# Moving the last block's output layer, its norms and the first GELU in a three-layer hybrid kernel

## The chip, the cores and the metric

The kernel runs on one core of a Trainium2 chip. A core has five engines that run at the same time, each through its own queue of instructions in a fixed order: TensorE (PE, with the loading of weights, PEld, shown apart), VectorE (DVE), ScalarE (ACT), GpSimd (POOL) and SyncE (SP), which here issues DMAs. An instruction waits for the results of others through semaphores, and whatever stands behind it on its engine waits with it.

The metric is the device time of one execution in microseconds (us), lower is better; several executions are timed and the median is given. One more execution is recorded by the hardware profiler.

## The reference

The input `x` has 4 sequences of 1024 tokens with 256 channels, in float32. Three layers follow, each added to `x`: a linear recurrent unit (LRU), a latent attention, and a sparse feed-forward layer that is applied before the attention and once more at the end. What the change touches is the end of the LRU and the beginning of the first sparse layer.

The end of the LRU, for one block of tokens (cut from the reference):

```python
out = out2[0] - out2[1] + o
y = gelu(out @ w1_w + w1_b)
y = y @ w2_w + w2_b + out
mean, var = y.mean(-1), y.var(-1)
y = (y - mean) * rsqrt(var + LN_EPS) * ln_g + ln_b      # then x = x + y
```

The sparse layer norms each token of `x` and takes a small grouped convolution of it (256 channels to 64); the result is normed a second time, over all 4096 tokens, by channel:

```python
xc = einsum('ngf,gf->ng', x2d.reshape(n, g, 4), conv_w) + conv_b
mean, var = xc.mean(0), ((xc - mean) ** 2).mean(0)
xa = gelu((xc - mean) * rsqrt(var + BN_EPS) * gamma + beta)
logits = xa @ lin_w.T + lin_b
```

Of the logits, made into weights by an exponential, each token keeps the largest (a top-k), once for its inputs and once for its outputs, around a dense product with a 256x256 matrix. The mean and variance over all tokens make a barrier: no GELU, and so no top-k, can start before the last token's convolution is done.

## The kernel before

The 4096 tokens lie in SBUF as 8 blocks of 512, each of 4 tiles of 128 tokens (32 tiles, `x[i]`). The program is written with a tile framework: its text gives the instructions and a priority by their order, and a scheduler sets the order on each engine from that and from a model of their durations. `tc.issue_after(ins)` adds a dependency by hand.

The stages lie in this order on the time axis. The LRU takes to about 257 us. For every block `Lru.outputs` makes the products `po` (L437, TensorE, moved by ACT to `ot`), the gate's first product `pz` (L443) with its GELU on ACT, the second product with its sum `ot` on VectorE (L455), the transposes `py` (L465, back to tokens on partitions), and the layer norm of `py`, after which the result is added to `x`. `layer_norm` (L124) takes `bn_stats` and `bn_aggr` of each view, then a reciprocal root by `rsqrt` on VectorE (L55 to L66: a guess by integer arithmetic and three Newton steps, tiny instructions one behind the other), and at last `shift` = -mean x rstd (L136). The normed value `yn` is one ACT instruction per tile with that scale and shift (L474); then `yn` x gain and `x` + `yn` (L479, L480), on GpSimd for most blocks. The last block is done in two halves of 256 tokens, to shorten the end, with these two on VectorE (`bufs` is set only there).

Beside the LRU run the heads of the first sparse layer, `Ffn.head` (L501), one for each block: `layer_norm` of `x`, then `normalized_t` (`xn` on ACT, L145, and its transposes `pt` on TensorE, L147), a copy `ft` of these (ACT, L524), its store to DRAM by SP (L527), the convolution `pc` (L529), `xc` (ACT, L533), and its statistics (VectorE, L534). The heads of blocks 0 to 3 lie in the LRU's loop. For the end of the loop the text has: head of block 4; three steps of the halves of the last block; head of block 5; the other steps; head of block 6 behind the last GELU of the LRU; and the two half heads of block 7 side by side.

Then `norm_scale` (L538) gathers the statistics of all blocks and makes from them scale `bs` and bias `bt` (tiny VectorE instructions, with the same root, L59 to L66). `gelu` (L585) is one ACT instruction per block of 512 tokens. `logits_product` (L551) gives `pl` for one tile, and `Ffn.tile` (L589) the top-k: MAX8 and MATCH_REPLACE8 on VectorE, in turns, all under the line L674, their order fixed by hand. The product with the dense matrix `pf` (L567, `full_product`) reads `tt`, the block's stored `ft`, loaded back by L561; later blocks make it ahead of time (`ahead`, `pfa`). The second product (`px`, L682, and L699) is made from the gated `xg` (L657, L658) and added to `x` (L662). `wfs` are the dense matrix in two parts for the more exact products later: a cast on ACT (L1151) and a difference on GpSimd (L1152). The weights of the attention (`attn_weights`, `wd`, `wqk`) are prepared beside the first tiles.

The first sparse layer's tiles 0 to 7 take 281 to 336 us. The attention, with tiles 8 to 31 of the first sparse layer and the heads of the second between its products, follows to about 1304 us, and the tiles of the second sparse layer end the run.

Of the kernel before, what the change touches and what calls it, by code (L numbers as in the profile page):

```python
# [10 lines left out]
F32 = mybir.dt.float32  # L11
# [5 lines left out]
ALU = mybir.AluOpType  # L17
# [4 lines left out]
P = 128  # L22
# [98 lines left out]
    return c, s, last  # L121


def layer_norm(nc, pool, tag, views, rstd=None, shift=None):  # L124

    n = len(views)
    mv = pool.tile([P, n, 2], F32, tag=f"{tag}_mv", name=f"{tag}_mv")
    if rstd is None:
        both = pool.tile([P, 2, n], F32, tag=f"{tag}_rs", name=f"{tag}_rs")
        rstd, shift = both[:, 0, :], both[:, 1, :]  # L130
    for i, v in enumerate(views):
        st = pool.tile([P, 6], F32, tag=f"{tag}_st", name=f"{tag}_st", bufs=4)
        nc.vector.bn_stats(st, v)
        nc.vector.bn_aggr(mv[:, i, :], st)
    rsqrt(nc, pool, tag, mv[:, :, 1], rstd)
    nc.vector.scalar_tensor_tensor(shift, mv[:, :, 0], -1.0, rstd, ALU.mult, ALU.mult)  # L136
    return rstd, shift


def normalized_t(nc, pool, psum, tag, ptag, views, rstd, shift, ident):  # L140

    pt = psum.tile([P, KD, len(views) * P], ptag, "pt")
    for i in range(len(views)):
        xn = pool.tile([P, D], F32, tag="fx_xn", name="xn", bufs=2)
        nc.scalar.activation(xn, views[i], AF.Identity, bias=shift[:, i : i + 1], scale=rstd[:, i : i + 1])  # L145
        for k in range(KD):
            nc.tensor.transpose(pt[:, k, i * P : (i + 1) * P], xn[:, k * P : (k + 1) * P], ident)  # L147
    return pt
# [46 lines left out]
class Lru:  # L195
# [226 lines left out]
    def outputs(self, r, xs, xnt, h, pairs, last, tag="po", bufs=None):  # L422

        nc, w, sp, vecs = self.nc, self.w, self.sp, self.vecs
        tiles = range(2 * pairs[0], 2 * pairs[-1] + 2)
        sl = slice(tiles[0] * P, (tiles[-1] + 1) * P)
        n = len(tiles) * P
        ot, zt = bufs or self.buffers()
        for c in range(KD):
            co = slice(c * P, (c + 1) * P)  # L430
            po = self.psum.tile([P, 512], tag, "po")[:, 0:n]
            self.inputs(po, r, 2, c, xnt, sl, stop=False)
            terms = [
                (self.w_mid[r][k][e][:, co], h[k][e][:, sl.start + r : sl.stop + r]) for k in range(KD) for e in range(2)
            ]
            for i, (lt, v) in enumerate(terms):
                nc.tensor.matmul(po, lt, v, start=False, stop=(i == len(terms) - 1))  # L437
            nc.scalar.activation(ot[:, c, :], po, AF.Identity, bias=self.ob[:, r, c : c + 1])
            yield
        for c in range(KD):  # L440
            pz = self.psum.tile([P, 512], "pu", "pz")[:, 0:n]
            for k in range(KD):
                nc.tensor.matmul(  # L443
                    pz, w[:, k, 2, c * P : (c + 1) * P], ot[:, k, :], start=(k == 0), stop=(k == KD - 1)
                )
            last_gelu = nc.scalar.activation(zt[:, c, :], pz, AF.Gelu, bias=vecs[:, V_B1 + c : V_B1 + c + 1])
        self.last_gelu = last_gelu.ins
        yield
        for c in range(KD):
            pz = self.psum.tile([P, 512], tag, "pz2")[:, 0:n]  # L450
            for k in range(KD):
                nc.tensor.matmul(
                    pz, w[:, k, 3, c * P : (c + 1) * P], zt[:, k, :], start=(k == 0), stop=(k == KD - 1)
                )
            nc.vector.scalar_tensor_tensor(  # L455
                ot[:, c, :], pz, vecs[:, V_B2 + c : V_B2 + c + 1], ot[:, c, :], ALU.add, ALU.add
            )
        yield
        pys = []
        for j in range(len(tiles) // 2):  # L460
            py = self.psum.tile([P, 2, D], "pu" if tag == "pu" else "py", "py")
            for i in range(2):
                tk = slice((2 * j + i) * P, (2 * j + i + 1) * P)
                for k in range(KD):
                    nc.tensor.transpose(py[:, i, k * P : (k + 1) * P], ot[:, k, tk], self.ident)  # L465
            pys += [py[:, 0, :], py[:, 1, :]]
        rstd, shift = layer_norm(nc, sp, f"ly{len(tiles)}", pys)
        gain, base = self.brow[:, 0, :], self.brow[:, 1, :]
        for q, tile_q in enumerate(tiles):
            xt = xs[tile_q]  # L470
            yn = sp.tile([P, D], F32, tag="yn", name="yn", bufs=3)
            if last:
                nc.gpsimd.tensor_tensor(xt, xt, base, ALU.add)
            self.last_yn = nc.scalar.activation(  # L474
                yn, pys[q], AF.Identity, bias=shift[:, q : q + 1], scale=rstd[:, q : q + 1]
            ).ins
            if last:
                engine = nc.vector if bufs else nc.gpsimd
                engine.tensor_tensor(yn, yn, gain, ALU.mult)  # L479
                engine.tensor_tensor(xt, xt, yn, ALU.add)  # L480
            else:
                nc.gpsimd.tensor_tensor(yn, yn, gain, ALU.mult)
                nc.gpsimd.tensor_tensor(yn, yn, base, ALU.add)
                nc.gpsimd.tensor_tensor(xt, xt, yn, ALU.add)
        yield


class Ffn:
# [9 lines left out]
        self.counted = 0  # L498
        self.dram, self.turned, self.full = None, {}, {}

    def head(self, blk, sp, psum, ptag, pairs=(0, 1), xtag="fx", ttag="ft"):  # L501


        nc, w = self.nc, self.w
# [14 lines left out]
        for i, j in enumerate(pairs):  # L519
            r = slice(2 * j, 2 * j + 2)  # L520
            xs = self.x[blk * 4 + 2 * j : blk * 4 + 2 * j + 2]
            pt = normalized_t(nc, sp, psum, xtag, ptag, xs, norm[:, 0, r], norm[:, 1, r], w.ident)
            tt = sp.tile([P, KD, 256], F32, tag=ttag, name="ft", bufs=2 if self.dram else 1)
            nc.scalar.copy(tt, pt)  # L524
            yield
            if self.dram:
                nc.sync.dma_start(self.turned[blk][:, :, j * 256 : (j + 1) * 256], tt)  # L527
            for k in range(KD):
                nc.tensor.matmul(  # L529
                    pc[k * 64 : (k + 1) * 64, i * 256 : (i + 1) * 256], w.cw[:, k, :], tt[:, k, :], start=True, stop=True  # L530
                )
# [6 lines left out]
    def norm_scale(self, sp):  # L538

        nc, w = self.nc, self.w  # L540
        bmv = sp.tile([P, 2], F32, tag="bmv", name="bmv")
        nc.vector.bn_aggr(bmv, self.bst[:, 0 : self.counted, :].rearrange("p a b -> p (a b)"))
        bs = self.bp.tile([P, 1], F32, tag="bs", name="bs", bufs=2)
        rsqrt(nc, sp, "bn", bmv[:, 1:2], bs)
        nc.vector.tensor_tensor(bs, bs, w.vecs[:, V_GAMMA : V_GAMMA + 1], ALU.mult)
        bt = self.bp.tile([P, 1], F32, tag="bt", name="bt", bufs=2)
        nc.vector.tensor_tensor(bt, bmv[:, 0:1], bs, ALU.mult)
        nc.vector.tensor_tensor(bt, w.vecs[:, V_BETA : V_BETA + 1], bt, ALU.subtract)
        self.bs, self.bt = bs, bt

    def logits_product(self, dst, i):  # L551
        nc, w = self.nc, self.w
# [29 lines left out]
            nc.sync.dma_start(self.full[blk][:, 2 * j : 2 * j + 2, :], v)  # L582
            yield

    def gelu(self, blk):  # L585
        x = self.xc[blk]
        return self.nc.scalar.activation(x, x, AF.Gelu, bias=self.bt, scale=self.bs).ins  # L587

    def tile(self, i, sp, psum, tags, out=None, fast=False, parts=None, tt=None, fine=False):  # L589
# [395 lines left out]
def run(*gens):  # L985
    for g in gens:
        for _ in g:
            pass
# [58 lines left out]
def tile_kernel(ctx: ExitStack, tc: tile.TileContext, x_in, w_lru, vecs_in, rows, w_ffn, lin_t, w_attn, w_down, out):  # L1047
# [34 lines left out]
    with ExitStack() as c1:  # L1082
# [16 lines left out]
        for k in range(NBLK):  # L1099
# [25 lines left out]
                h[b].append(lru.states(xnt[b * CH : (b + 1) * CH], c))  # L1125
            if 2 <= k < NBLK - 2:
                run(f1.head(k - 2, lru.sp, psum, "pt"))
        for blk in range(4, NBLK - 3):
            run(f1.head(blk, lru.sp, psum, "pt"))
        k = NBLK - 1  # L1130
        ot, zt = lru.buffers()
        halves = [
            lru.outputs(k % CH, xb[k], xnt[k], h[k // CH], (i,), last, tag, [v[:, :, c : c + 256] for v in (ot, zt)])
            for i, tag, c in ((0, "pu", 0), (1, "po", 256))
        ]
        for i in (0, 0, 1):
            next(halves[i])
        run(f1.head(NBLK - 3, lru.sp, psum, "pt"))
        for i in (0, 1, 0, 1, 0, 1, 1):
            next(halves[i])  # L1140
        with tc.issue_after(lru.last_gelu):
            run(f1.head(NBLK - 2, lru.sp, psum, "pt"))
        run(*(f1.head(NBLK - 1, lru.sp, psum, "pu", (i,), "lx", "zt") for i in range(2)))

    with ExitStack() as c2:
        sp = c2.enter_context(tc.tile_pool(name="at_s", bufs=2))
# [2 lines left out]
        wqk, wvo, wd = two([P, KD, HEADS * HD], "wqk"), two([P, PAIRS, D], "wvo"), two([P, KD, P], "wd")  # L1149
        wfs = two([P, KD, D], "wf")  # L1150
        nc.scalar.copy(wfs[0], w.wf)  # L1151
        nc.gpsimd.tensor_tensor(wfs[1], w.wf, wfs[0].bitcast(F32), ALU.subtract)  # L1152
        at = Attention(tc, x, ident, ident64, wqk, wvo, wd, sp, wp)
        with ExitStack() as c4:
            psum = Banks(
# [1 line left out]
            )  # L1157
            fp = c4.enter_context(tc.tile_pool(name="f_t", bufs=4))
            weights = attn_weights(nc, fp, psum, "at", w_attn, w_down, wqk, wvo, wd, at, ident64)
            f1.norm_scale(sp)  # L1160
            tts = [f1.load(blk, fp, f"tt{blk}") for blk in range(2)]
            f1.gelu(0)
            with tc.issue_after(f1.gelu(1)):
                warm(nc, sp, AF.Exp)
            tiles = [
# [174 lines left out]
```

## Time and profile before

| | us |
|---|---|
| median of 3 runs | 1511.01 (1509.11 to 1512.66) |
| profiled execution | 1507.37 |
| its span, first instruction to last | 1505.6 |
| mean granted TensorE clock in it | 0.952 of full speed |

A row of the timeline gives the start from the span's start, the length, the engine, the line of the kernel, the operation, and what it writes and reads with the shape; `x4` says that the row stands for four such instructions, and a bracket at the end how long the engine had been idle before and what released it. These rows are the middle of the end of the LRU (second half of the last block), from its last sum to the statistics of `x`:

```profile
255.34 0.47 DVE L455 SCALAR_TENSOR_TENSOR ot<-pz,vecs,ot 128x256 f32<-128x256 f32 x1
255.41 1.01 PE L465 MATMUL py<-ident,ot 128*128 128x128 f32 x4 [0.37 <-DVE ot L455]
...
256.45 0.76 DVE L133 BATCH_NORM_STATS2 ly_st<-py 128x6 f32<-128x256 f32 x2
...
260.95 1.02 ACT L474 ACTIVATE yn<-py,ly_rs 128x256 f32<-128x256 f32 x2
...
262.95 0.42 DVE L480 TENSOR_TENSOR x<-x,yn 128x256 f32<-128x256 f32 x1
...
263.68 0.42 DVE L133 BATCH_NORM_STATS2 fx_st<-x 128x6 f32<-128x256 f32 x1
...
266.08 1.09 ACT L145 ACTIVATE xn<-x,norm_f 128x256 f32<-128x256 f32 x2 [0.30 <-DVE norm_f L136]
```

In the table of windows a row gives a stretch and its length, the busy time of PE, PEld, DVE, ACT and POOL with the number of instructions, the granted clock of TensorE, the busy share of the DMA engines, and GB/s.

### The profile page before, as it was taken

What the parts mean: (1) busy time and instruction counts of PE and PEld (TensorE: products, weight loads), DVE (VectorE), ACT (ScalarE), POOL (GpSimd) and SP (SyncE); (2) the same over time, 40 slices, a digit from 0 to 9 for tenths busy, and PEclk for the clock granted to TensorE, in tenths of its full rate; (3) what the DMA queues carried; (4) which work ended last, traced back from release to release, by engine and by line L of the source; (5) the groups of instructions that cost most, each with busy time, mean ns of one, the idle gap of its engine ahead of it and who ended that gap; (6) DMA issues with size and microseconds to landing.
All of it is one profiled execution on the core that took longest, in us unless ns stands there. A gap on an engine that the chain in (4) does not pass through costs nothing. (4 is left out here: it accounts for less than half of the span.)

```text
span 1505.6 us, 28728 instructions
## 1 busy us (share of the span) xinstructions
PE 1278.4 (85%) x10136; PEld 947.3 (63%) x10136; DVE 1181.0 (78%) x3682; ACT 1018.0 (68%) x2152; POOL 683.0 (45%) x849
## 2 busy tenths in 40 slices
PE   4899998887998998898988988889999999576765
PEld 3645555465776777676766766677777877244544
DVE  8988676796778876977777778777676675599998
ACT  5334535666878877787877687877877776566664
POOL 2024523352555454454534543545443534067776
PEclk9999999799999999999999999999999999678898
DMA  3010000432553443353434344433444444000000
GB/s 119 20 55 15 22 21 29 144 105 50 92 88 72 81 86 67 61 89 75 77 73 79 61 69 80 75 74 71 71 85 85 85 85 85 1 15 25 22 25 29
DMA packets 288754, 96.52 MB, mean 64 GB/s; under 512 B 268377, under 2 KB 284770, under 8 KB 288610
## 3 DMA queue, kind: packets, MB, share of 16 engines
q1 hardware_dynamic: 283522, 88.90, 29.6%
q10 hardware_dynamic: 5088, 5.78, 1.1%
q8 instruction: 80, 1.31, 0.4%
q14 instruction: 64, 0.52, 0.1%
HBM read 16.01 MB, written 11.53 MB: 18 GB/s over the span
## 5 line engine op out<-in xcount | busy, mean ns | idle before, releaser
L898 POOL TENSOR_TENSOR pd<-pr,pd 128x1024 f16<-128x1024 f32 x128 | 273.6, 2142 | 259.3 <-ACT pd L897 200.1
L890 DVE TENSOR_REDUCE nm<-sc 128x1 f32<-128x1024 f32 x256 | 308.4, 1217 | 74.8 <-PE sc L886 73.2
L894 ACT ACTIVATE pr<-sc,nm 128x1024 f32<-128x1024 f32 x256 | 286.1, 1120 | 89.8 <-DVE nm L892 54.7
L886 PE MATMUL sc<-kh,qs 128*128 128x512 f32 x512 | 184.4, 438 | 28.5 <-ACT pr L894 21.0
L886 PE MATMUL sc<-kl,qs 128*128 128x512 f32 x512 | 161.7, 396 | 0.0
L674 DVE MATCH_REPLACE8 wk<-m,wk 128x256 f32<-128x256 f32 x384 | 155.3, 408 | 0.1
L910 ACT COPY p<-ptp 128x512 f32<-128x512 f32 x224 | 124.1, 591 | 44.4 <-PE ptp L905 32.5
L674 DVE MAX8 m<-wk 128x8 f32<-128x256 f32 x384 | 150.7, 413 | 0.4
L905 PE MATMUL ptp<-ident,pr 128*128 128x128 f32 x1024 | 139.2, 276 | 13.3 <-ACT pr L894 12.0
L930 PE MATMUL pmo<-p,la 128*64 128x128 f32 x2048 | 140.2, 284 | 5.9 <-ACT ft L524 2.9
L905 PEld LDWEIGHTS ptp<-ident,pr 128*128 128x128 f32 x1024 | 116.2, 141 | 35.5 <-ACT pr L894 21.7
L897 ACT CAST pd<-pr 128x1024 f16<-128x1024 f32 x128 | 133.5, 1054 | 4.6 <-DMA d<-pd 3.6
L930 PEld LDWEIGHTS pmo<-p,la 128*64 128x64 f32 x2048 | 119.6, 142 | 24.7 <-issue 4.7
L886 PEld LDWEIGHTS sc<-kh,qs 128*128 128x128 f32 x512 | 85.2, 195 | 53.9 <-ACT pr L894 32.9
L886 PEld LDWEIGHTS sc<-kl,qs 128*128 128x128 f32 x512 | 96.6, 189 | 23.2 <-issue 1.4
L930 PE MATMUL pmo<-d,lb 128*64 128x128 f16 x3072 | 101.5, 220 | 8.7 <-DVE qs L853 2.6
L930 PEld LDWEIGHTS <-lb 128*64 128x64 f16 x3072 | 90.7, 110 | 26.6 <-issue 19.9
L628 POOL TENSOR_TENSOR ex<-ex,wk 128x512 f32<-128x512 f32 x61 | 77.8, 1276 | 58.4 <-DVE wk L674 48.9
L926 POOL COPY rows<-rs 128x128 f32<-128x128 f32 x128 | 36.3, 297 | 120.4 <-PE pmo L938 71.7
L941 DVE TENSOR_TENSOR on<-pmo,rb 128x128 f32<-128x128 f32 x128 | 36.4, 284 | 64.8 <-ACT rb L940 64.3
L147 PE MATMUL pt<-ident,xn 128*128 128x128 f32 x256 | 48.9, 310 | 44.0 <-ACT xn L145 32.3
L699 PE MATMUL pf<-wf,vt 128*128 128x256 f32 x288 | 80.9, 424 | 3.9 <-ACT vt L697 3.4
(307 smaller groups left out, 2766.1 us busy)
## 6 DMA issues: line engine op xcount, KB each, us to landing
tt<-ft SPq DMA_DIRECT2D x16, 256.0 KB
tt<-tt SPq DMA_DIRECT2D x8, 512.0 KB
out<-x SPq DMA_DIRECT2D x32, 128.0 KB
x<-in_x ACTq DMA_DIRECT2D x6, 512.0 KB
pf<-pfs SPq DMA_DIRECT2D x12, 256.0 KB
full<-pf SPq DMA_DIRECT2D x24, 128.0 KB
d<-pd SPq DMA_TRANSPOSE x128
wa<-in_w_attn SPq DMA_DIRECT2D x2, 640.0 KB
```

Of the source, the lines that this page charges most:

```text
L147: nc.tensor.transpose(pt[:, k, i * P : (i + 1) * P], xn[:, k * P : (k + 1) * P], ident)
L628: pool.tensor_tensor(ex, ex, wk, ALU.subtract)
L674: ins = make(*args).ins
L699: nc.tensor.matmul(dst, vt[:, k, :], w.wf[:, k, :], start=(k == 0 and bias is None), stop=(k == KD - 1))
L886: nc.tensor.matmul(sc[:, sl], qs[:, j, q * P : (q + 1) * P], kk[:, sl], start=(i == 0), stop=(i == 1))
L890: nc.vector.tensor_reduce(nm, sc, AX.X, ALU.max, negate=True)
L894: nc.scalar.activation(pr, sc, AF.Exp, bias=nm, accum_out=ssum[:, j : j + 1])
L897: nc.scalar.copy(pd[:, 0, :], pr)
L898: nc.gpsimd.tensor_tensor(pd[:, 1, :], pr, pd[:, 0, :], ALU.subtract)
L905: nc.tensor.transpose(pt[:, kk, :], pr[:, kc * P : (kc + 1) * P], self.ident)
L910: nc.scalar.copy(dst, pt)
L930: nc.tensor.matmul(po[j * HD : (j + 1) * HD, 0, :], v, pts[j][:, c, :], start=(n == 0), stop=(n == len(terms) - 1),)
```

## The change

In the text of the program, all steps of the last block's two halves now stand directly behind the loop, and the heads of blocks 4, 5 and 6 behind them; the dependency of block 6's head on the last GELU is gone. For the last block's halves the norm is written as two VectorE instructions per tile: `yn` = (`py` - mean) x gain, and `x` = `yn` x rstd + `x`; `shift` is not made there, and ACT's `yn` and the two instructions of L479 and L480 are left out. In the heads of blocks 6 and 7 `xn` is made by VectorE (`tensor_scalar` with two operands per partition) instead of ACT. The GELU of block 0 is one instruction of 128 tokens and one of 384. The difference `wfs[1]` on GpSimd waits for the last instruction of `norm_scale`.

```diff
-def layer_norm(nc, pool, tag, views, rstd=None, shift=None):
+def layer_norm(nc, pool, tag, views, rstd=None, shift=None, mean=False):
...
     rsqrt(nc, pool, tag, mv[:, :, 1], rstd)
+    if mean:
+        return rstd, mv[:, :, 0]
     nc.vector.scalar_tensor_tensor(shift, mv[:, :, 0], -1.0, rstd, ALU.mult, ALU.mult)
...
         xn = pool.tile([P, D], F32, tag="fx_xn", name="xn", bufs=2)
-        nc.scalar.activation(xn, views[i], AF.Identity, bias=shift[:, i : i + 1], scale=rstd[:, i : i + 1])
+        if fast:
+            nc.vector.tensor_scalar(xn, views[i], rstd[:, i : i + 1], shift[:, i : i + 1], ALU.mult, ALU.add)
+        else:
+            nc.scalar.activation(xn, views[i], AF.Identity, bias=shift[:, i : i + 1], scale=rstd[:, i : i + 1])
...
-        rstd, shift = layer_norm(nc, sp, f"ly{len(tiles)}", pys)
+        rstd, shift = layer_norm(nc, sp, f"ly{len(tiles)}", pys, mean=bufs is not None)
...
             if last:
                 nc.gpsimd.tensor_tensor(xt, xt, base, ALU.add)
+            if bufs:
+
+                mean = shift[:, q : q + 1]
+                nc.vector.scalar_tensor_tensor(yn, pys[q], mean, gain, ALU.subtract, ALU.mult)
+                nc.vector.scalar_tensor_tensor(xt, yn, rstd[:, q : q + 1], xt, ALU.mult, ALU.add)
+                continue
...
             if last:
-                engine = nc.vector if bufs else nc.gpsimd
-                engine.tensor_tensor(yn, yn, gain, ALU.mult)
-                engine.tensor_tensor(xt, xt, yn, ALU.add)
+                nc.gpsimd.tensor_tensor(yn, yn, gain, ALU.mult)
+                nc.gpsimd.tensor_tensor(xt, xt, yn, ALU.add)
...
-        nc.vector.tensor_tensor(bt, w.vecs[:, V_BETA : V_BETA + 1], bt, ALU.subtract)
         self.bs, self.bt = bs, bt
+        return nc.vector.tensor_tensor(bt, w.vecs[:, V_BETA : V_BETA + 1], bt, ALU.subtract).ins
...
-    def gelu(self, blk):
-        x = self.xc[blk]
+    def gelu(self, blk, tokens=slice(0, 512)):
+        x = self.xc[blk][:, tokens]
...
-        for blk in range(4, NBLK - 3):
-            run(f1.head(blk, lru.sp, psum, "pt"))
...
-        for i in (0, 0, 1):
+        for i in (0, 0, 1, 0, 1, 0, 1, 0, 1, 1):
             next(halves[i])
-        run(f1.head(NBLK - 3, lru.sp, psum, "pt"))
-        for i in (0, 1, 0, 1, 0, 1, 1):
-            next(halves[i])
-        with tc.issue_after(lru.last_gelu):
-            run(f1.head(NBLK - 2, lru.sp, psum, "pt"))
-        run(*(f1.head(NBLK - 1, lru.sp, psum, "pu", (i,), "lx", "zt") for i in range(2)))
+        for blk in range(4, NBLK - 1):
+            run(f1.head(blk, lru.sp, psum, "pt", fast=blk == NBLK - 2))
+        run(*(f1.head(NBLK - 1, lru.sp, psum, "pu", (i,), "lx", "zt", True) for i in range(2)))
...
-        nc.gpsimd.tensor_tensor(wfs[1], w.wf, wfs[0].bitcast(F32), ALU.subtract)
...
-            f1.norm_scale(sp)
+            with tc.issue_after(f1.norm_scale(sp)):
+                nc.gpsimd.tensor_tensor(wfs[1], w.wf, wfs[0].bitcast(F32), ALU.subtract)
...
-            f1.gelu(0)
+            for tokens in (slice(0, P), slice(P, 512)):
+                f1.gelu(0, tokens)
```

The scheduler places every instruction anew from the changed text. In the order that results, each engine runs nearly the same number of instructions (VectorE 3178 for 3172, ScalarE 1773 for 1784, the others the same), but some places differ that the diff doesn't name: at the start of the sparse layer's tiles TensorE runs `pl` of tile 0, then four `pf` instructions, then `pl` of tile 1 (before: both `pl`, then the `pf`); at the end of tile 7 the transposes `px` stand ahead of `pfa`; and in the attention and the last layer some neighbours have changed places.

## The prediction

> **What bounds the kernel now.** I read the table of busy shares, then the costliest groups, then the wait before single instructions in three stretches, and last the windows by stage. No engine is full over the whole run (the page's first section):
>
> ```profile
> PE 1278.4 (85%) x10136; PEld 947.3 (63%) x10136; DVE 1181.0 (78%) x3682; ACT 1018.0 (68%) x2152; POOL 683.0 (45%) x849
> ```
>
> So each stage has to be asked by itself. The windows (sum of the stretch, then busy PE, PEld, DVE, ACT, POOL, the granted clock, DMA share and rate) around the place of the change:
>
> ```profile
> 240.00:252.00 12.00, 12.00 (x71) 10.03 (x68) 5.78 (x27) 7.26 (x16) 5.00 (x8) 1.00 0.06 22
> 252.00:262.00 10.00, 5.04 (x25) 2.97 (x24) 9.36 (x58) 4.20 (x9) 0.53 (x1) 0.94 0.08 28
> 262.00:274.00 12.00, 8.30 (x30) 3.48 (x30) 6.37 (x38) 6.71 (x13) 0.13 (x2) 0.50 0.26 88
> 274.00:281.00 7.00, 2.77 (x4) 1.17 (x4) 3.60 (x14) 3.62 (x5) 1.36 (x2) 0.50 0.83 272
> 281.00:290.00 9.00, 9.00 (x47) 7.00 (x46) 6.91 (x34) 6.12 (x19) 2.29 (x7) 0.79 0.46 184
> 290.00:336.00 46.00, 38.84 (x174) 28.42 (x174) 46.00 (x202) 30.94 (x77) 29.19 (x41) 0.96 0.31 104
> ```
>
> To 252 us TensorE is full (12.00 of 12.00). From 252 to 281 nobody is: a chain of short steps, at half clock on TensorE from 261 on. From 290 to 336 VectorE is full (46.00 of 46.00, the top-k of tiles 0 to 7). The change works on the chain of 252 to 281; what it saves there counts only if VectorE's full stretch starts earlier, since that stretch and all behind it keep their length. The end of the chain, in the timeline (start, length, engine, line):
>
> ```profile
> 272.79 0.47 ACT L533 ACTIVATE xc_f<-pc,vecs 128x256 f32<-128x256 f32 x1 [1.22 <-PE pc L529]
> 273.30 0.43 DVE L534 BATCH_NORM_STATS2 bst_f<-xc_f 128x6 f32<-128x256 f32 x1 [2.41 <-ACT xc_f L533]
> ...
> 274.80 1.26 POOL L1152 TENSOR_TENSOR wf<-wf,wf 128x512 fp32r<-128x512 f32 x1 [0.18 <-ACT wf L1151]
> 274.94 1.13 DVE L66 SCALAR_TENSOR_TENSOR bs<-bn_t,bs 128x1 f32<-128x1 f32 x1
> ...
> 276.42 0.16 DVE L66 SCALAR_TENSOR_TENSOR bs<-bn_t,bs 128x1 f32<-128x1 f32 x1
> ...
> 277.70 1.52 ACT L587 ACTIVATE xc_f<-xc_f,bt,bs 128x512 f32<-128x512 f32 x2 [2.98 <-DVE bt L548]
> ...
> 278.56 3.78 PE L556 MATMUL pl<-lint,xc_f 128*128 128x512 f32 x4 [4.24 <-ACT xc_f L587]
> ...
> 280.67 0.76 DVE L674 MAX8 m<-pl 128x8 f32<-128x256 f32 x2 [3.01 <-PE pl L556]
> ...
> 282.38 0.76 DVE L674 MAX8 m<-pl 128x8 f32<-128x256 f32 x2 [0.94 <-PE pl L556]
> ```
>
> Each step waits for the one above; the two rows of L66 are the same operation on 128x1, once 1.13 and once 0.16 us.
>
> **The change part by part**, as differences to that execution.
>
> *Outputs first.* The instructions of the last block before head 4 to 6 in the text become, on TensorE, little: the conv of block 4 goes behind `po` of half 0, the transposes of block 5 behind `po` of half 1, and what stands ahead of the last `py` transposes (255.41) is nearly the same set. TensorE is full before that, so a permutation of the same work gains 0. The heads' stores (L527, 256 KB each on SP's queue) go with their heads and keep their order; on POOL only the adds of `base` come a place earlier, in a queue that idles from 252 on. It costs on VectorE: two of the new `yn` instructions (0.47 by the row of L455, the same kind and shape) and the 128x512 statistics of block 5 (0.69) come ahead of the last L455, at a rate of 0.39 + 0.39 + 0.6 less what lay idle there (0.4): about +1.0 us for `py` of half 1. Bounds 0 and +1.6; I take +1.0.
>
> *Norms on VectorE.* Half 1 goes today 258.69 (shift) to ACT `yn` at 260.95 (ACT is busy with `xn` until then), L479, L480 at 262.95. After: no shift (a step of 0.2), no ACT round trip, and two 128x256 instructions with 0.47 each. From reciprocal root ready (260.04) two pairs need 1.6 to 1.9 us: x complete at about 262.0 instead of 263.4, so -1.4. Against it stand four `xn` of block 6 on VectorE: four times 0.35 (the row of TENSOR_SCALAR 128x256 with two operands per lane, L269/L270, 348 ns; ACT's L145 takes 597), 1.1 to 1.4 us, that come in between. For block 7, 0.35 for 0.6 plus a wait for ACT: two in a row, twice, -0.4 each. Sum of the part: -1.4 + 1.2 - 0.5, about -0.7. With outputs first, the last statistics (273.30) move by +1.0 - 0.7 = +0.3, bounds -1.0 and +1.3.
>
> Here a rule speaks against the change. The Trainium skill, "GPSIMD Engine Reference", section 8, says that GpSimd shares its way into SBUF with VectorE and that the two stand in each other's way when VectorE runs in a two-port mode or reads two SBUF operands; f32 `tensor_scalar` from SBUF is of that kind ("VectorE: DVE Perf Modes"). By the rule the eight new `xn` could be stalled by POOL, each by up to a POOL instruction (1.26, as the 1.13 of L66 shows). The row says that POOL is busy for 0.53 us in 252 to 262 and 0.13 in 262 to 274: nothing to meet. By rule +1 or more, by row 0; I take 0. The same two rows price the next part.
>
> *wf1 behind the scale.* L1152 no longer lies beside L66: 1.13 becomes 0.16, -0.97. It then runs about 276.9 to 278.1, where VectorE waits for logits, and `wfs[1]` is read only by later stages; nothing is queued behind it on POOL but `nm` of tile 0, due after the first MAX8 (281.53 today). Bounds 0 (it hits another instruction) and -0.97; I take -0.97.
>
> *GELU of 128.* ACT's 128x512 takes 0.76, 128x256 0.47; by the same slope 128x128 is about 0.34. `pl` of tile 0 starts 0.4 earlier. One instruction more on ACT hides behind TensorE. All told `pl(0)` starts at 278.56 + 0.3 - 0.97 - 0.4 = 277.5.
>
> *What that triggers.* TensorE's order at this place also changes: today `pl(0)`, `pl(1)`, then four `pf` (L567, eight records); after, `pl(0)`, `pf` x4, `pl(1)`. At half clock a `pf` record takes 0.427 (the mean of the rows at 281 to 285), so 3.4 us for eight. `pl(0)` runs 277.5 to 279.2, `pf` to 282.6, then `pl(1)`. When it ends is a matter of the clock. The Trainium skill, "TensorE: Matmul & The Clock Gate", Part 1, has full speed after some 3.4 us of sustained work (about 4). The row differs: TensorE works without a gap from 278.56, yet the granted clock is 0.50 to 284, 0.64 in the next microsecond and 1.00 from 285, some 6 us on. By the rule the clock is full from 281, `pf` ends at 281.9, `pl(1)` at 282.7: MAX8 of tile 1 0.3 later than today's 282.38. By the row the clock is full from 283.5, and `pl(1)` ends at 283.9: 1.5 later. The order of the top-k is fixed, so tile 0's rounds stand behind this MAX8. Against it goes what VectorE idles today in front of L630 at 286.18: 1.15 us, tile 1's exponentials being late behind POOL's work on `wd`. The third tile (289.95) then moves by -0.8 by the rule, +0.4 by the row. I take the row, bounds -0.8 and +1.5 (the idle stays).
>
> *Tail of tile 7.* Today its `px` transposes wait behind eight `pfa` of a later block, although their input `xg` (L658, 0.96 us from 337.65) is there at 338.6:
>
> ```profile
> 339.20 1.89 PE L567 MATMUL pfa<-wf,tt 128*128 128x256 f32 x8
> ...
> 340.93 0.38 PE L682 MATMUL px<-ident,xg 128*128 128x128 f32 x2
> ```
>
> After, `px` stands in front of these `pfa`: up to -2.2; but the product L699 now stands behind six `pml` (1.99 at 344.21). I take -1.2, between -2.2 and 0.
>
> *The rest.* Later swaps (around tile 12, in the last layer) move equal work about. The last layer holds VectorE at 20.00 of each 20 us from 1370 to 1490: its sum doesn't change. 0, by -2 to +2.
>
> **Sum.** The -1.1 of `pl(0)` is spent at the start of VectorE's full stretch, which begins +0.4 later; tail -1.2; rest 0: **-0.8**. On the profiled execution, 1507.37 (span 1505.6 and 1.8 around it), that gives 1506.6; this execution was 3.6 below the median of 1511.01, so the forecast for a median is 1511.0 - 0.8 = **1510.2**.
>
> **Rivals.** *B, all of it pays.* The clock rises while `pf` runs (-0.8), the heads end 1.0 earlier and the DMA of `tt` with them (-1.0), tail -2.2, and the swapped orders behind bring 1.0: -5.0, **1506**. For it: three measured stalls (0.97, 1.15, 2.2) lie there to be taken. Against: the `pf` in front of `pl(1)`.
>
> *C, slower: the wait for `tt` takes the place of the wait for GELU.* `pf` x4 reads block 0's turned activations, loaded by a DMA issued at 274.15. By the bytes that the DMA rows show from then on (1.05 MB by 278.3, both `tt` loads), it lands about 278.5 if the queue serves in order, just ahead of `pl(0)`'s end. If it is served beside the weights behind it, it lands by 281.5, and `pl(1)` is behind it: 281.5 + 3.4 + 1.7 = 286.6, MAX8 of tile 1 4.2 late, 3.2 after the idle: **1514.2**. It decides from a landing after 279.2, one for one. Against it: today's first `pf`, at 281.28, shows no wait for a DMA.
>
> *D, it doesn't do what it says*: the scheduler keeps TensorE's order, the last `py` come no earlier, and wf1's stall returns at another instruction: **1511**.
>
> **How the numbers follow.** 0.2%, about what can be told from no change, is 3.0 us. A, the forecast, 0.41 (with a spread of 3: faster 0.11, same 0.25, slower 0.05); B 0.30 (0.28, 0.02, 0); C 0.19 (0, 0.03, 0.16); D 0.10 (0.02, 0.07, 0.01). Faster 0.41, same 0.37, slower 0.22. The range, 1503.5 to 1515.5, takes in B and C with their spread of 1 to 2 us; A alone is 1507 to 1513.5.
>
> **What would show it.** Right: the L66 rows all 0.16; first MAX8 near 279.5; second near 284 with a wait for `pl`; third tile about 290.4; `px` of tile 7 near 339. Wrong: a long L66 or a `pf` waiting for DMA; statistics of block 7 outside 272.3 to 274.6; a second MAX8 before 283 (then B); or a difference of over 3 us that arises behind 360.

## The result, and the profile after

The changed kernel takes 1524.24 us in the median of 6 runs (1521.27 to 1530.30), the kernel before 1511.86 in as many (1509.11 to 1517.19): a ratio of 1.0081, with a 95% interval of 1.0059 to 1.0103. The forecast was 1510.2, within 1503.5 to 1515.5. It is 12 us slower, where 0.8 faster was forecast. Of the signs that the prediction named for being wrong, three came: a long L66 (1.14 us), statistics of block 7 outside 272.3 to 274.6 (274.72), and more than 3 us that arise behind 360.

The profiled execution took 1521.90 us, its span 1520.2: 14.6 more than the one before. The table cuts both spans at points that every kernel here has; all lengths are worked out from the two timelines.

| stretch | before | after | difference |
|---|---|---|---|
| start to the statistics of block 3 (L534) | 215.5 | 215.3 | -0.2 |
| to the last statistics of block 7 | 57.8 | 59.4 | +1.6 |
| to the first logits (L556) | 5.3 | 5.0 | -0.3 |
| to the MAX8 of tile 1 | 3.8 | 6.1 | +2.3 |
| to the last top-k instruction of tile 7 | 53.4 | 56.4 | +3.0 |
| to the first maximum of the attention (L890) | 22.9 | 22.7 | -0.2 |
| to its last one | 912.0 | 921.3 | +9.3 |
| to the second norm over all tokens | 29.9 | 30.0 | 0.0 |
| to the end | 205.1 | 204.0 | -1.0 |

The timeline of the changed kernel at the end of the LRU, in the columns used above (its line numbers are up to 14 higher):

```profile
256.81 0.55 PE L471 MATMUL py<-ident,ot 128*128 128x128 f32 x3 [0.72 <-DVE ot L461]
...
261.78 0.15 DVE L139 SCALAR_TENSOR_TENSOR norm_f<-fx_mv,norm_f 128x4 f32<-128x4 f32 x1
...
262.07 0.72 DVE L149 TENSOR_SCALAR xn<-x,norm_f 128x256 f32<-128x256 f32 x2
...
263.71 0.15 DVE L66 SCALAR_TENSOR_TENSOR ly_rs<-ly_t,ly_rs 128x2 f32<-128x2 f32 x1
...
264.17 0.87 DVE L484 SCALAR_TENSOR_TENSOR x<-yn,ly_rs,x 128x256 f32<-128x256 f32 x2
...
274.72 0.43 DVE L545 BATCH_NORM_STATS2 bst_f<-xc_f 128x6 f32<-128x256 f32 x1 [2.47 <-ACT xc_f L544]
...
276.22 1.26 POOL L1166 TENSOR_TENSOR wf<-wf,wf 128x512 fp32r<-128x512 f32 x1 [0.18 <-ACT wf L1157]
276.36 1.14 DVE L66 SCALAR_TENSOR_TENSOR bs<-bn_t,bs 128x1 f32<-128x1 f32 x1
...
279.13 1.79 ACT L598 ACTIVATE xc_f<-xc_f,bt,bs 128x128 f32<-128x128 f32 x3 [2.98 <-DVE bt L560]
...
279.67 2.08 PE L567 MATMUL pl<-lint,xc_f 128*128 128x512 f32 x2 [3.92 <-ACT xc_f L598]
...
281.54 3.36 PE L578 MATMUL pf<-wf,tt 128*128 128x256 f32 x8
...
284.74 1.02 PE L567 MATMUL pl<-lint,xc_f 128*128 128x512 f32 x2
...
285.80 0.77 DVE L685 MAX8 m<-pl 128x8 f32<-128x256 f32 x2 [1.52 <-PE pl L567]
...
292.11 0.75 DVE L685 MAX8 m<-pl 128x8 f32<-128x256 f32 x2
```

Three things are to be seen. The shift of block 6's norm (L139) comes at 261.78, 3 us behind its old place (258.76), because VectorE has other instructions in its queue (counted from the statistics of block 3, outputs first alone makes 0.7 of this, e1; the new norm in the old order 1.9, e2); and the last two `x` of the LRU (L484) stand behind block 6's `xn`. The difference on GpSimd still runs at 276.22, ahead of `bt`, and beside it L66 still takes 1.14 us. And the logits of tile 1 come at 284.74, behind eight records of `pf`.

The windows are cut here on a grid of 3.41 us (length, then PE, PEld, DVE, ACT, POOL busy, granted clock, DMA share, GB/s). First before, around the end of tile 7's top-k, then after:

```profile
325.67:329.09 3.42, 1.99 (x8) 1.44 (x8) 3.42 (x19) 3.41 (x5) 0.00 (x0) 1.00 0.23 87
329.09:332.50 3.41, 1.34 (x6) 1.22 (x7) 3.41 (x11) 3.38 (x6) 2.59 (x3) 1.00 0.00 0
332.50:335.91 3.41, 3.16 (x9) 1.89 (x8) 3.41 (x19) 1.84 (x5) 0.81 (x2) 0.50 0.36 141
335.91:339.33 3.42, 3.42 (x21) 3.05 (x20) 2.95 (x7) 2.03 (x5) 1.68 (x2) 1.00 0.04 15
```

```profile
328.87:332.29 3.42, 1.64 (x9) 1.19 (x7) 3.42 (x20) 3.41 (x5) 0.39 (x1) 1.00 0.02 5
332.29:335.70 3.41, 0.00 (x0) 0.00 (x0) 3.41 (x14) 3.39 (x6) 1.71 (x2) 1.00 0.00 0
335.70:339.11 3.41, 2.80 (x7) 2.16 (x8) 2.93 (x14) 3.20 (x8) 0.41 (x2) 0.50 0.40 154
339.11:342.53 3.42, 3.42 (x12) 2.86 (x12) 2.11 (x9) 1.64 (x4) 1.31 (x2) 0.50 0.01 2
```

The clock goes to exactly half for whole windows of this grid, here behind a window in which TensorE was busy for less than half. Before, that is one window (1.34 busy). After, TensorE does nothing for a whole one, and two windows follow at half clock: the first of the two, busy for 2.80 of 3.41, does not bring the full clock back. A window busy for 1.64 kept it, so half is no sharp limit (the last section counts the cases). The timeline says why:

```profile
329.95 4.34 ACT L598 ACTIVATE xc_f<-xc_f,bt,bs 128x512 f32<-128x512 f32 x6
...
335.69 1.05 ACT L592 COPY pfs<-pfa 128x512 f32<-128x512 f32 x2
...
336.31 2.08 PE L578 MATMUL pf<-wf,tt 128*128 128x256 f32 x4 [5.80 <-ACT pfs L592]
...
338.39 1.91 PE L710 MATMUL pf<-wf,vt 128*128 128x256 f32 x4
...
340.42 0.42 DVE L673 TENSOR_TENSOR x<-x,pf 128x256 f32<-128x256 f32 x1 [1.79 <-PE pf L710]
```

ScalarE is taken for 7 us by the GELUs of blocks 2 to 7 and two loads of function tables. In the changed order TensorE has its `pfa` products done when this starts, and waits 5.80 us for ScalarE to empty the buffers. The products behind run at half clock (L710 1.91; 1.03 at 336.17 before), and VectorE, which was full in this stretch, waits 1.79 for them. That is most of its idle time between the MAX8 of tile 1 and the last top-k instruction of tile 7, 2.5 us where it was 1.2 before. The rest of the 3.0 us is work: VectorE is busy for 53.9 us there instead of 52.3, since the changed order has put other instructions (L673 is one) ahead of that last one, and the stretch behind is only 0.2 shorter for it.

The same windows lie all over the attention: 7 at half clock before, 14 after. The experiments have to say what of this the change does, and what is chance.

### The profile page after: what moved, and what is told of

Its sections match the earlier page's. It is cut to its first block, busy times and chain, and to the rows that moved or that the text cites. A ratio compares the mean times of both kernels' runs of the same rounds, so it can differ in the third digit from the quotient of the medians.

```text
span 1520.2 us, 28735 instructions
## 1 busy us (share of the span) xinstructions
PE 1295.1 (85%) x10136; PEld 962.9 (63%) x10136; DVE 1185.6 (78%) x3688; ACT 1013.5 (67%) x2141; POOL 682.5 (45%) x849
## 5 line engine op out<-in xcount | busy, mean ns | idle before, releaser
L685 DVE MATCH_REPLACE8 wk<-m,wk 128x256 f32<-128x256 f32 x384 | 158.7, 419 | 0.1
L941 PE MATMUL pmo<-p,la 128*64 128x128 f32 x2048 | 144.9, 289 | 5.4 <-ACT ft L535 2.9
L941 PEld LDWEIGHTS pmo<-p,la 128*64 128x64 f32 x2048 | 123.6, 145 | 25.0 <-issue 5.1
L710 PE MATMUL pf<-wf,vt 128*128 128x256 f32 x288 | 82.6, 433 | 3.2 <-ACT vt L708 2.9
```

The source lines that it names most:

```text
L685: ins = make(*args).ins
L710: nc.tensor.matmul(dst, vt[:, k, :], w.wf[:, k, :], start=(k == 0 and bias is None), stop=(k == KD - 1))
L941: nc.tensor.matmul(po[j * HD : (j + 1) * HD, 0, :], v, pts[j][:, c, :], start=(n == 0), stop=(n == len(terms) - 1),)
```

## The experiments

For every run the same stretches were taken from its timeline; "half" is the number of half-clock windows of 3.41 us in the attention (first to last L890). The ratio is to the kernel before on the same chip.

| kernel | ratio (95%) | heads | to MAX8 of tile 1 | top-k | attention | half |
|---|---|---|---|---|---|---|
| before | 1 | 57.8 | 3.8 | 53.4 | 912.0 | 7 |
| after | 1.0081 (1.0059 to 1.0103) | 59.4 | 6.1 | 56.4 | 921.3 | 14 |
| e1 outputs first | 1.0015 (0.9996 to 1.0034) | 59.0 | 3.8 | 53.3 | 913.8 | 10 |
| e2 norms | 1.0021 (0.9999 to 1.0044) | 59.0 | 3.8 | 56.5 | 918.6 | 11 |
| e3 GELU of 128 | 1.0044 (1.0023 to 1.0064) | 57.8 | 5.3 | 59.9 | 918.7 | 11 |
| e4 delay | 1.0043 (1.0016 to 1.0071) | 57.8 | 3.8 | 56.7 | 911.0 | 7 |
| e5 GELU, order kept | 0.9993 (0.9974 to 1.0012) | 57.8 | 3.5 | 53.7 | 916.3 | 10 |
| e6 after, order kept | 1.0043 (1.0025 to 1.0061) | 59.4 | 3.5 | 53.5 | 919.2 | 12 |
| e7 wf1 held | 0.9999 (0.9981 to 1.0017) | 57.8 | 3.8 | 52.9 | 915.1 | 9 |
| e8 after, both held | 1.0043 (1.0024 to 1.0061) | 59.4 | 3.8 | 54.2 | 923.2 | 15 |
| e9 e6 without norms | 1.0020 (1.0001 to 1.0039) | 59.1 | 3.8 | 54.8 | 917.8 | 11 |
| e10 e6, xn of block 6 on ACT | 1.0024 (1.0011 to 1.0037) | 57.6 | 3.7 | 53.6 | 918.0 | 11 |
| e11 clock kept, heads | 1.0084 (1.0065 to 1.0104) | 58.5 | 2.0 | 59.5 | 920.5 | 11 |

(e12, the kernel of e11 with more of the same, is at 1.0124, 1.0103 to 1.0145.) The lengths are those of one execution each, the ratios those of 6 to 12 against 6 to 35. The first stretch, to the statistics of block 3, is left out: it takes 215.3 to 216.3 us, but 218.0 to 219.4 in the traces of e3, e6, e10 and e12, which have half-clock windows near 157 us. That e3 has them, whose edit lies behind this stretch, says that they are chance.

### The parts alone: e1, e2, e3, and a delay: e4

```diff
# e1: the steps of the last block's halves all together, heads 4 to 6 behind them (as in the change; xn stays on ACT)
# e2: mean=True path, and fast=True for heads 6 and 7, in the old order
# e3: for tokens in (slice(0, P), slice(P, 512)): f1.gelu(0, tokens)
# e4, in norm_scale of the first sparse layer:
+        for _ in range(6 if self.tag == "f1" else 0):
+            nc.vector.tensor_scalar(bmv, bmv, 1.0, None, ALU.mult)
```

> The kernel before with one part of the change: all steps of the last block's outputs ahead of the heads of blocks 4 to 6. Theory G (the loss comes mostly from half-clock windows on TensorE, 3.4 us each on a fixed grid, that follow a window in which TensorE was busy less than about half): statistics of block 7 within 1 us of 273.3, second MAX8 within 1 us of 282.4; the time then follows the count of half-clock windows between 285 and 1290 us, 9 before and 21 after, at about 1.2 us each. Theory D (a later start of the top-k carries through and nothing else): time within 1 us of before plus the shift of the second MAX8.

> The kernel before with one part of the change: the last block's norm and the xn of blocks 6 and 7 on VectorE. If VectorE is what makes the heads late, statistics of block 7 come 1 to 2 us later than 273.3 (1.4 after); if the order of the outputs does it, they come at 273.3 or up to 1.5 earlier. Theory G: the time is before plus that, plus 1.2 us for each half-clock window between 285 and 1290 above 9. Theory D: before plus the shift of the second MAX8, to 1 us.

> The kernel before with one part of the change: the GELU of block 0 as 128 and 384 tokens. First logits 0.3 to 0.4 us earlier than 278.56. If the split alone brings the four products of the dense matrix ahead of the second tile's logits, the second MAX8 comes 1.5 to 2.5 later than 282.4. Theory G: time by the count of half-clock windows, 1.2 us each above or below 9; theory D: before plus the shift of the second MAX8, to 1 us.

> The kernel before with six tiny VectorE instructions more in the norm over all tokens (a multiplication of the statistics by 1), about 1.2 us; the engines' orders in the attention stay nearly those of before. Theory D: time before plus 1.2 us, to 2. Theory G: the delay moves the work against the grid of clock windows, the count of half-clock windows between 285 and 1290 changes from 9, and the time moves by 1.2 us for each of them, so it can be 5 or more away from before plus 1.2.

Measured: e1 1514.26, e2 1515.39, e3 1519.29, e4 1516.30 us against 1512.23. The medians of the three parts add up to what the whole costs (0.15 + 0.21 + 0.44 against 0.81%), each known to 0.2, and more than half comes from the smallest of them, one ACT instruction cut in two. Theory D fails: e3's loss is far above any late start (second MAX8 1.1 late once its later LRU is taken off). Theory G is not settled by e4. Its trace has the 7 windows of before and an attention of 911.0, but that execution took 1510.02, near the lowest of ten (1508.95 to 1523.39); against the profiled execution of before (1507.37) it is 2.7 us slower with as many windows in the attention. What differs there is 1.2 for the delay, 3.3 in the column "top-k", and less behind it. The new thing is this column, which I had taken for a stretch of fixed length: 53.4 in before and e1, but 56 to 60 in e2, e3 and e4. In e3 it is this row on VectorE:

```profile
306.52 0.17 DVE L630 RECIPROCAL rs<-ssum 128x2 f32<-128x2 f32 x1 [3.62 <-ACT ex L615]
```

A wait of 3.62 us inside the "full" stretch. In e2, e3 and e4 the scheduler, moved by a small edit, has put the work of tiles 0 to 7 in another order on all four engines. Compared row by row with before, from 5 us ahead of the first logits to the attention, 43 of TensorE's 318 products and 56 of VectorE's 302 instructions stand at another place in e3, as many in the changed kernel, 17 and 45 in e2, 23 and 45 in e4; in e1 it is 1 and 0.

### The order of the dense products: e5 and e6

```diff
                 pf = psum.tile([P, D], tags[2], "pf")
-                self.full_product(pf, tt, q)
+                with self.tc.issue_after(self.last_logits) if i < 2 else nullcontext():
+                    self.full_product(pf, tt, q)
```

e5 is e3 with this, e6 the changed kernel with it.

> The kernel before with the GELU of 128 and 384 tokens, and with the first two dense products held behind the second tile's logits on TensorE, so that the orders of all engines are those of before. Theory O (what the split of the GELU cost, +6.6 us alone, is the order that the scheduler makes of it: dense products ahead of the second tile's logits and all that is moved behind): within 1.5 us of before, first logits 0.3 earlier. Theory I (the split itself costs: an ACT instruction more, a later GELU of the other 384): 4 us or more above before.

> The changed kernel with the first two dense products held behind the second tile's logits on TensorE. Theory O: it loses the GELU part of the loss, so 5 to 8 us less than the changed kernel's 1524.2, that is about 1517.5 (before plus 2.3 for the order of outputs plus 3.2 for the norms), second MAX8 near 284. Theory C (the wait is only moved, tile 0's work was what filled VectorE): within 2 us of 1524.

Measured: e5 1510.60 against 1511.51, e6 1518.88. Theory O holds in both. With the split GELU and this hold, every engine's order is that of before save a few places (at most 4 per engine in this stretch), and the loss of e3 is gone: the same edit is 0.44% above before without the hold and 0.07% below with it. In the changed kernel the hold takes away 2.6 us to the MAX8 of tile 1 and 2.9 of the top-k, and the time falls by as much (ratio 1.0081 to 1.0043, 5.7 us; the two intervals allow 1.4 to 10). What became of the stretch ahead of tile 7 in e6:

```profile
330.73 4.34 ACT L598 ACTIVATE xc_f<-xc_f,bt,bs 128x512 f32<-128x512 f32 x6
330.75 1.99 PE L578 MATMUL pfa<-wf,tt 128*128 128x256 f32 x8 [1.58 <-DVE x L674]
...
335.48 1.99 PE L578 MATMUL pfa<-wf,tt 128*128 128x256 f32 x8 [2.74 <-ACT ob L662]
...
338.23 1.13 PE L578 MATMUL pf<-wf,tt 128*128 128x256 f32 x4 [0.76 <-ACT pfs L592]
```

The `pfa` products are again left for the time in which ScalarE is busy, the idle time is in pieces of 1.58, 2.74 and 0.76 us, and the product of tile 7 takes 1.13 instead of 2.08.

### The difference on GpSimd: e7 and e8

```diff
-        nc.gpsimd.tensor_tensor(wfs[1], w.wf, wfs[0].bitcast(F32), ALU.subtract)
...
             next(tiles[0])
+            with tc.issue_after(f1.last_nm):
+                nc.gpsimd.tensor_tensor(wfs[1], w.wf, wfs[0].bitcast(F32), ALU.subtract)
```

`last_nm` is the GpSimd instruction that needs the first MAX8. e7 is before with this, e8 is e6 with it.

> The kernel before with the difference of the dense matrix on GpSimd queued behind the first instruction of GpSimd that needs the first MAX8, so that it can't start ahead of the scale. If its place beside the scale is what makes one tiny VectorE instruction take 1.13 us, that one takes 0.16 and the first logits come 1.0 us earlier than the statistics allow before (5.26 us after the start of block 7's last statistics; 4.3 here). The time then: 0 to 1.5 below before. If something else stalls it, 1.13 stays.

> The changed kernel with both holds: the dense products behind the second tile's logits, and the difference on GpSimd behind the first MAX8. First logits 4.0 us after the start of block 7's last statistics (4.95 in the changed kernel). Theory: 0 to 1.5 us below e6, so about 1516.5; still 3 or more above before, since the heads stay late.

Measured: e7 1511.21 against 1511.51, e8 1519.57. The cause of the stall is shown: e7's timeline has

```profile
274.84 0.16 DVE L66 SCALAR_TENSOR_TENSOR bs<-bn_t,bs 128x1 f32<-128x1 f32 x1
...
277.49 3.73 PE L556 MATMUL pl<-lint,xc_f 128*128 128x512 f32 x4 [3.69 <-ACT xc_f L587]
```

0.16 in place of 1.13, and first logits 4.3 us after the last statistics in place of 5.3. But the microsecond is not found in the time: 0.9999, and e8 is no faster than e6. A microsecond is 0.07% of the time, and the intervals reach 0.18% to either side: a gain of this size is less than these runs can tell.

### What makes the heads late: e9 and e10

e9 is e6 with all norms as before; e10 is e6 with `xn` of block 6 on ScalarE:

```diff
-            run(f1.head(blk, lru.sp, psum, "pt", fast=blk == NBLK - 2))
+            run(f1.head(blk, lru.sp, psum, "pt"))
```

> The changed kernel with the dense products held behind the second tile's logits, and with all norms back as before (yn, xn on ScalarE, gain and sum as before). The norms alone on the kernel before cost 3.2 us, the order alone 2.3. If the parts add, this is 0 to 2.5 us above before, about 1513, and 5 below the 1518.9 of the changed kernel with the hold. If the norms only cost because of the order they stand in, or the order is what costs, it stays within 2 of 1518.9.

> The changed kernel with the dense products held behind the second tile's logits, and with xn of block 6 back on ScalarE; the last block's norm and the xn of block 7 stay on VectorE. If the four xn of block 6 make the heads late (they stand in VectorE's queue ahead of the sum of the last tiles), the statistics of block 7 come 1.0 to 1.5 us earlier against the stage in front than in the changed kernel, and the time falls by as much, to about 1517. If the two instructions of yn and x per tile make them late, statistics and time stay within 0.5 and 2.

Measured: e9 1517.24, e10 1517.14 against 1513.76. The heads take 59.1 us in e9 and 57.6 in e10, against 59.4 in e6. Not all of these 1.8 us are the `xn` of block 6: the last sum `x` of the LRU is ready 1.3 earlier in e10, and the other 0.5 is the clock, which happened to be full in e10 for the last convolution:

```profile
274.49 0.65 PE L540 MATMUL pc<-ft,cw 128*64 128x256 f32 x4 [0.68 <-ACT ft L535]
```

In e6 it takes 1.12. So four `xn` on VectorE make 1.3 us of lateness, outputs first makes 1.2 by itself (e1, e9: 1.2 and 1.3), and the last block's new norm and block 7's `xn` win most of that back where block 6's `xn` stays away (e10: 0.3 late at equal clock). Both stay some 0.2% above before. Of the 9.7 us between e9's trace and that of before 1.3 are late heads, 1.4 a longer top-k and 5.8 the attention; in e10's the start is 2.6 longer (half clock near 157 us) and the attention 6.0.

### The clock kept up: e11 and e12

```diff
+def keep(tc, w, psum, tag, after, n):
+    with tc.issue_after(after):
+        pk = psum.tile([P, 512], tag, "pk")
+        for _ in range(n):
+            tc.nc.tensor.matmul(pk, w.ones, w.linb, start=True, stop=True)
...
+        keep(tc, w, psum, "po", lru.last_py, 14)
...
+            keep(tc, w, psum, "at", f1.last_pc, 14)
```

> The kernel before with 28 matrix products whose result is read by nobody: 14 behind the last transposes of the LRU and 14 behind the last convolution of block 7, about 3 us each at full clock, both where TensorE idles over 4 us. Theory G (a window of 3.4 us with TensorE under half busy halves the clock): the seven half-clock windows at 261 to 285 us go to 0 to 2, the transposes and convolutions of blocks 6 and 7 take 0.6 instead of 1.1 us, statistics of block 7 come 3 to 4.5 us earlier (about 269.5), first logits 4 to 5 earlier; time 2 to 5 below before. Theory T (the clock rows are a record of something else): the clock stays 0.5 there, and the 28 products, at 0.43 us each, make the first logits 2 or more late.

> As the one before, with three more groups of 14 such products at the end of the attention: behind the output products of the last tiles (two) and behind the last convolution. Theory G: the seven half-clock windows at 1285 to 1309 us go to 0 to 3 as well, the start of the second sparse layer comes 3 to 5 us earlier, time 4 to 9 below before. Theory T: 0 or slower.

Measured: 1526.59 and 1533.31 against 1513.76, so theory G's forecast fails, though the clock moves its way: of seven half-clock windows between 261 and 285 us four are left (0 to 2 were forecast). Windows of e11:

```profile
252.00:262.00 10.00, 8.37 (x42) 4.55 (x40) 8.86 (x56) 3.89 (x8) 1.14 (x2) 1.00 0.08 28
...
264.00:270.00 6.00, 3.48 (x16) 1.36 (x12) 4.15 (x29) 3.38 (x7) 0.00 (x0) 0.55 0.25 87
...
278.00:281.00 3.00, 3.00 (x12) 1.31 (x11) 0.91 (x5) 1.91 (x3) 0.00 (x0) 0.96 0.98 396
```

The first group of products holds off the half clock to 264.7 (261 before), the second brings the full clock back at 278.4 (284.7), and both tiles' logits take 1.98 us instead of 3.78. But the heads are no earlier (58.5): between 260 and 264 TensorE had 1.23 us of work in 4, and the clock fell all the same. And the scheduler, with 28 instructions more, chose another order for tiles 0 to 7: VectorE waits 4.5 us once for ScalarE's exponentials, and the top-k takes 59.5. In e12 the half-clock windows at the end of the attention go from 7 to 2, and the stretch there from 29.9 to 29.3 only: its chain hardly hangs on TensorE's clock.

A run that would have filled the 5.8 us ahead of tile 7 in the changed kernel with such products, and one that would have left outputs first out of e6, were not made.

## Why the prediction was wrong, point by point

**Outputs first and norms: +0.3 forecast, +1.6 measured.** Counted from the statistics of block 3, the terms came out so: the last transposes `py` end 1.2 late (+1.0 forecast); from there to the last sum `x` the new norm wins 0.6 (e10), where a gain of 1.4 was put; the four `xn` of block 6 cost 1.3 (e10 against e6; +1.2 put); and the `xn` of block 7 win 0.3 (0.5 put). The mis-sized term is the gain of the norm. Its step was "from reciprocal root ready (260.04)": it took the root to be ready when it was before, but for the later `py`.

```profile
259.89 0.15 DVE L66 SCALAR_TENSOR_TENSOR ly_rs<-ly_t,ly_rs 128x2 f32<-128x2 f32 x1
```

From the end of `py` to the ready root it is 3.6 us in this trace of before (256.42 to 260.04) and 6.5 in the changed kernel (257.36 to 263.86), and VectorE is busy for 6.4 of the 6.5. It is 4.9 with outputs first alone (e1), 5.5 in e10, 6.5 in e6. That from 252 to 281 no engine is full did not hold for VectorE: the prediction's own row has it busy for 9.36 of 10 us from 252 to 262, so what is put there pushes the small steps of the root back. That POOL would not meet the `xn` held: they take 0.36 to 0.41 us.

**wf1: -0.97 forecast, 0 measured.** The size was right (e7), the step was not: "L1152 no longer lies beside L66". It does. In these runs `issue_after` orders only the queue of the engine that the named instruction is on, here VectorE: the GpSimd instruction inside the block ran at 276.22, 2.7 us ahead of the named one (278.93), and was held in e7, where the named one is on GpSimd too. Rival D had named a return of this stall, at another instruction. Even held, it brought nothing that the runs could tell.

**GELU of 128: -0.4 forecast, -0.3 measured** (and in e5 and e6).

**Dense products ahead of the second logits: +0.4 forecast.** The local sum held: TensorE goes from `pl(0)` through eight `pf` records, MAX8 of tile 1 waits; it is 2.3 late against `pl(0)`, where the sum made 2.5 of it (1.1 earlier, 1.5 later). The idle time in front of L630 paid for a part, as forecast: in the trace of before the MAX8 of tile 2 is

```profile
289.95 0.73 DVE L674 MAX8 m<-pl 128x8 f32<-128x256 f32 x2
```

which is 7.57 us behind that of tile 1 (282.38). After, it is 6.31 (285.80 to 292.11), 1.26 less, where 1.15 was put. The step that failed is the frame of the whole: that VectorE's full stretch "and all behind it keep their length". From the MAX8 of tile 2 to that of tile 7 it is 0.9 longer, 0.7 of it one wait for an exponential, and from there to tile 7's last top-k instruction 3.3 (17.1 us instead of 13.8), where TensorE has its idle 5.80. Together with the loss at the start, this one order is worth 5.7 us of the 12 (e6), 7.7 in e3 against e5.

**Tail of tile 7: -1.2 forecast, -0.2 measured.** The step read the order wrongly, and so does the description of the change: no `px` has moved ahead of `pfa`. Counted in the two traces, the `px` of tile 6 stand behind 80 records of `pfa` and those of tile 7 (346.7 us) behind 96, before and after. It is sixteen `pfa` that have moved ahead, to the front of tile 5's `px` (80 instead of 64). So TensorE had none left for the time of the GELUs, and this opened the 5.80 us of idle time.

**The rest: 0, by -2 to +2.** "Later swaps move equal work about" is the other step that did not hold. The attention is 9.3 us longer in the profiled pair, though there only 46 of VectorE's 1714 instructions stand at another place. Over the 13 traces of the table its length follows the number of half-clock windows, 1.5 us for each, with a correlation of 0.94; what remains of it is 1.2 us. This is no proof of a cause, since a wait that keeps TensorE idle makes both. And the number is partly chance: e5 and e7 have the order of before in the attention (at most 2 instructions of an engine elsewhere), and their traces show 10 and 9 windows and 916.3 and 915.1 us.

The whole kernel shows the same: 35 executions of the kernel before range from 1506.93 to 1521.26 us, and their times fall by 0.8 us for each 0.001 of mean granted clock (correlation -0.86). Both profiled executions were lucky ones. That of before, with 7 windows and 0.952 (mean of the 35: 0.946), lies 4 to 5 us below the medians of its kernel, that of the changed kernel, with 0.942 (mean of its six: 0.936), 2.3; so some 2 of the 14.6 us between them are luck. The mean of 0.936 is below those of all the other kernels (0.942 to 0.948). At 0.8 us for 0.001 that is 7 to 8 us of the 12, part of it the windows ahead of the attention (2 before, 7 after), so it overlaps with what the order of tiles 0 to 7 costs. This is a reckoning from the spread, not a run that set the clock, and elsewhere it fails: e4, e9 and e10 have mean clocks of 0.947, 0.946 and 0.945, where before has 0.945 on the same chips, and are 3.4 to 4.1 us slower.

**Rivals.** C named the right place and the wrong mechanism: `pf` ahead of `pl(1)`, but no wait for `tt`, and a price of 3 where it was 6. No rival had the order of eight tiles change as a whole.

**Open.** What is left in e6 without late heads (e10, 0.24%, 0.11 to 0.37) has no shown cause. In e10's trace it comes with a longer attention and 11 windows at half clock, but the mean clock of its 12 executions is no lower than before's. Its order in the attention is the most changed of all (151 of VectorE's 1714 instructions elsewhere, 225 of TensorE's 8243); no run held that order. Nor is it shown directly that the half clock behind the 5.8 us costs what the rows suggest. No version was found that is faster than before: e5 and e7 can't be told from it.

## What to carry to other kernels

Where a scheduler orders the work from its own model of time, an edit's price is not in its own instructions: the same cut of one instruction cost 0.44% freely, and nothing that could be told with two products held in place. Compare the order of every engine before and after, follow each swap to what it leaves idle and when, and hold the order by hand when only the edit is to be measured. And before summing against one profiled execution, look where it lies among the executions of the same kernel.

## What the runs showed of the hardware

The granted clock is 0.50 or 1.00, in stretches that are whole multiples of 3.41 us, and the grid of these lies differently against the start in every execution (from 0.5 to 3.4 us, modulo 3.41). The Trainium skill, "TensorE: Matmul & The Clock Gate", Part 1, has it so: a window of 3.413 us that runs freely. What it calls an idle window need not be idle. In the changed kernel's attention (windows as above):

```profile
445.00:448.40 3.40, 1.71 (x11) 0.99 (x9) 3.40 (x11) 3.40 (x9) 1.97 (x2) 0.99 0.00 0
448.40:451.80 3.40, 3.40 (x33) 3.22 (x32) 3.40 (x15) 1.78 (x3) 1.92 (x2) 0.51 0.58 110
```

A window busy for half is followed by one at half clock. Here is the count over all windows from 30 us on of the fourteen traces, by TensorE's busy share in a window (the profile's, in which the ends of products are modelled) and the clock of the window behind it:

| busy share | at full clock: half follows | at half clock: full follows |
|---|---|---|
| under 0.4 | 208 of 208 | 0 of 109 |
| 0.4 to 0.5 | 77 of 138 | 0 of 24 |
| 0.5 to 0.7 | 50 of 571 | 0 of 74 |
| 0.7 to 0.9 | 3 of 914 | 27 of 131 |
| 0.9 and more | 7 of 3564 | 313 of 331 |

So less work keeps the clock up than brings it back. This fits the rise in the prediction's row that came some 6 us after TensorE had begun (278.56): the window from 277.89 was busy for 0.80, the next one wholly, and the clock is full from 284.71.

The seven cases of the last row's first count lie at one place. At 291.3 us in the changed kernel the clock falls for two windows behind one in which TensorE was busy without a gap, mostly with 64x64 products of the attention's weights, and in the other six traces the window in front holds 23 to 32 of these products too. That they count for less is a guess; no run took them away.
